# Layer 1's q and k in a two-layer fp32 kernel: dense products placed in strips by transfers, and one group's squares on ScalarE

## The chip, the cores and the metric

The kernel runs on one core of a Trainium2 chip. The metric is device time in microseconds from launch to end; lower is better. Three runs of the kernel before gave 1683.4, 1684.3 and 1684.37 us, median 1684.3. A profile page describes one further execution.

The engines have short names here. PE is TensorE (PEld its weight loads), DVE is VectorE, ACT is ScalarE, POOL is GpSimd, and SP is the engine whose queue issues nearly all transfers. PSUM is the memory into which PE writes its products.

## The reference

The input is x, 16 images of 512 tokens with 128 features, all fp32. Two layers follow each other. Both normalise, and both add an attention branch and a feed-forward branch to x:

```
xn = layernorm(x)
x  = x + linear_attention(xn) + mixture_of_experts(xn)      # layer 0
xn = layernorm(x)
x  = x + chunked_attention(xn) + channel_mix(xn)            # layer 1
```

Layer 0's attention is linear and causal, with 16 heads of 8 features and rotary positions. Its mixture of experts sends each token to 2 of 8 experts (128 -> 512 -> 128, with squared relu between) and adds a shared expert of the same shape.

Layer 1's attention is what the change is about:

```
q, k, v = xn @ W_qkv.T           # 16 heads of 8 features
for each chunk of 64 queries:    # keys up to the chunk's end
    p   = softmax(q k^T / sqrt(8))
    p   = p * (0.5 + 0.5 * gate(sum of p));  p = p / sum(p)
    out = p v
```

## The kernel before

**An order planned at build time.** The code does not run its loops in order. Generators describe the work; each call on an engine records an operation, and `Program.run` lays the operations out in an order with a list scheduler: it keeps a clock for each of the five engines, prices each operation by `COSTS` and by simple rules in `Program.call` (80 ns for an issue on SP, with an assumed landing 2 us later plus bytes at 250 GB/s), and emits what can start first, the lower index first among those. What is emitted is the fixed order of each engine. So changed work or a changed price moves the order of everything after it. All recorded operations have one line in the profile, L259, and groups are told apart by the names of their tiles. `Base` records who writes and reads a tile, `Slots` the buffers of a tag.

**Stages.** The 16 images go in five groups of 3, 4, 4, 3 and 2 (`GROUPS`). For each group, `dispatch` normalises and routes, and POOL scatters the token rows to their experts' slots in DRAM; `slot_tiles` fetches an expert's weights for each tile of 128 slots (`wf` and `wp`, 256 KB each, four buffers each) and computes hidden and output rows; `layer0` does linear attention and the shared expert; `layer1` does layer 1 image by image. These chains are woven together, so that experts and layer 0 of one group lie beside layer 1 of the group before.

**Experts' tiles** (`hidden`): a product `hg_ps`, a relu on ACT into `hg`, the square of `hg` in place, and the second product `yg_ps`. The square runs on POOL for the first pair of a quad and on DVE for the second; in group 0 always on DVE.

**Layer 1 of one image b.** `head(b)` loads x1, adds the experts' rows to it, normalises it into `xp`, runs `channel_mix` and `values`, and then `operands` for the first half of the heads (u=0). `body(b)` runs `weighted` for u=0 with `operands` of u=1 beside it, then `weighted` for u=1 with `head(b+1)` beside it.

A matmul here contracts over at most 32 rows for each of four strips of the PE array. A strip j holds two heads (16 rows of features), then rows that carry the running maximum and the mask. So `operands` wants q and k in strips of 32 partitions with 16 rows of data: `wqk1` is padded with zero columns accordingly, one product for each u and for each of q and k (`qk`), and DVE adds the constant rows while it moves the product out of PSUM: one addition for `qa`, and two for `ka` (one for each head of a pair, with `parity` clearing the other head's rows). Then come the scores `sc` in five units, whose maxima DVE takes into `maxima`; PE transposes these (`mx`), and DVE subtracts them from `qa` in place. `weighted` computes `st` from `ka` and `qa`, ACT the exponential `ex`, and PE the product `o` with the values. The tags `qa` and `ka` have two buffers. In group 0, `layer0` runs images 0 and 1 side by side, and the second borrows these buffers (`LENT`).

Of the kernel before, what the change touches and what calls it, by code (L numbers as in the profile page):

```python
# [29 lines left out]
F32 = mybir.dt.float32  # L30
# [6 lines left out]
P = 128  # L37
# [15 lines left out]
def slot_count(gt):  # L53
# [29 lines left out]
_CONST = (  # L83
    ("ident", P), ("cos", NT * 4), ("sin", NT * 4), ("blocks", 8 * (PAIR + 2)), ("pick", 4),
    ("causal", P), ("rank", E), ("upper", P), ("ones", P), ("tile", SLOT_TILES),
    ("aug_q", T), ("aug_k", 2 * T), ("parity", 2),
)


# [68 lines left out]
class Base:  # L158


    def __init__(self, slots, make):
        self.slots, self.make, self.tile = slots, make, None
        self.writers, self.readers = [], []
        self.left, self.free_at, self.users = 0, 0.0, []

    def made(self):
# [58 lines left out]
class Program:  # L225
# [21 lines left out]
    def call(self, name, api, method, args, kw):  # L247
        views = [a for a in (*args, *kw.values()) if isinstance(a, View)]
        o = kw.get("out", args[0] if args else None)
        writes = [o.base] if isinstance(o, View) else []  # L250
        reads = [v.base for v in views if v is not o]
        n = math.prod(o.shape[1:]) if isinstance(o, View) else 0
        later = 0.0

        def made(a):
            return a.made() if isinstance(a, View) else a

        def emit():
            return getattr(api, method)(*map(made, args), **{k: made(a) for k, a in kw.items()})  # L259

        if name == "PE":
            later = 60.0
            form = (args[1].shape[0], o.shape[0])
            if method == "transpose":
                cost = 112.0
            elif args[1].shape[0] == 32:
                cost = max(0.425 * n, 56.0)
            elif o.shape[0] == 32:
                cost = max(0.425 * n, 56.0)
            else:  # L270
                cost = max(1.68 * n, 224.0)
        elif method == "dma_start":
            cost, later = 80.0, 512.0 * n
        else:
            form = method if (name, method) in COSTS else None
            if name == "DVE" and method in ("tensor_scalar", "tensor_scalar_min", "tensor_scalar_max"):
                form = "fast"
            if method in ("tensor_reduce", "bn_stats"):
                n = math.prod(args[1].shape[1:])
            least, each = COSTS[name, form]  # L280
            cost = least + each * n
            if kw.get("func", args[2] if len(args) > 2 else None) == AF.Sqrt:
                cost += 2600.0
        op = self.add(name, emit, reads, writes, cost, later)
        if name == "PE":
            (self.unit_of[0] if self.unit_of else op).form = form
        return op

    def add(self, name, emit, reads, writes, cost, later=0.0):
        if self.unit_of is not None:  # L290
            if self.unit_of == []:
                self.unit_of.append(self._new(name, None, 0.0, 0.0))
            op = self.unit_of[0]
            part = Op(name, emit, 0.0, 0.0, op.index)
            op.parts.append(part)
            op.cost += cost
        else:
            part = op = self._new(name, emit, cost, later)
        for base in reads:
            op.needs.update(base.writers)  # L300
        for base in writes:

            op.needs.update(o for o in base.writers if o.engine != "SP" or name != "SP")
            op.needs.update(base.readers)
        for base in reads:
            base.readers.append(op)
        for base in writes:
            if base.readers:
                base.writers, base.readers = [], []
            base.writers.append(op)  # L310
        op.needs.discard(op)
        op.bases.update(reads, writes)
        op.wrote.update(writes)
        return part
# [172 lines left out]
def two_layers(ctx: ExitStack, tc: tile.TileContext, x, small, const, w_fc, w_proj, out):  # L487
# [22 lines left out]
    def big(name):  # L510
        return ps_big.tile([P, 2, 512], F32, tag="big", name=name)
# [6 lines left out]
        i.behind = [(first, mybir.DependencyClass.NoSync)]  # L518


    const_sb = fixed.tile([P, _CONST_N], F32, tag="const", name="const_sb")
    small_sb = fixed.tile([P, _STAYS_N], F32, tag="small", name="small_sb")

    wfc_s = fixed.tile([P, FF], F32, tag="wfc_s", name="wfc_s")
# [13 lines left out]
    lo = _CONST_AT["aug_q"][0]  # L538
    SP.dma_start(const_sb[:, 0:lo], const[:, 0:lo])
    raw = {}  # L540
    for name in ("wqkv0", "wqk1"):
        program.lag = 400 if name == "wqk1" else 0
# [3 lines left out]
    for names in (_STAYS[:2], _STAYS[2:]):  # L546
# [4 lines left out]
    lo = _CONST_AT["aug_q"][0]  # L551
    SP.dma_start(const_sb[:, lo:], const[:, lo:])
    program.lag = 250
    SP.dma_start(wfc_s, w_fc[:, E, :])
    SP.dma_start(wpj_s, w_proj[:, E, :, :])
# [2 lines left out]
    def c_(name):  # L558
        lo, hi = _CONST_AT[name]
        return const_sb[:, lo:hi]  # L560
# [19 lines left out]
    aug_k = c_("aug_k").rearrange("p (o t) -> p o t", o=2)  # L580
# [541 lines left out]
    def slot_tiles(g):  # L1122
# [41 lines left out]
        def hidden(xgT, ws, q, pair):  # L1164
            ph = big(f"hg_ps_{g}_{q}_{pair}")
            for ii, (wf, _) in enumerate(ws):
                i = 2 * pair + ii
                for f in range(NF):
                    M.matmul(
                        ph[:, ii, f * P : (f + 1) * P], wf[:, f * P : (f + 1) * P],  # L1170
                        xgT[:, i * P : (i + 1) * P], start=True, stop=True,
                    )
            h = p2.tile([P, 2, FF], F32, tag="hid", name=f"hg_{g}_{q}_{pair}", bufs=4)
            o = h[:, 0 : len(ws), :]
            S.activation(o, ph[:, 0 : len(ws), :], AF.Relu)

            (V if pair or g == 0 else G).tensor_tensor(o, o, o, ALU.mult)
            return h

        def project(h, ws, n):  # L1180
# [110 lines left out]
            )  # L1291
        return vp

    def operands(xT, b, u):
# [20 lines left out]
        yield  # L1315
        mx = maxima
        for i, unit in enumerate(QUERIES):
# [192 lines left out]
    def head(b):  # L1510

        if not 0 <= b < B:
            return None
        x1 = p2.tile([P, NT, D], F32, tag="x1", name=f"x1_{b}")
        assert passed["x1", b].base.writers
        SP.dma_start(x1.rearrange("p t d -> p (t d)"), passed["x1", b])
        yield from combine(x1, b)
        xp = p2.tile([P, T + 1], F32, tag="xp", name=f"xp_{b}", bufs=2)
        G.memset(xp[:, 0:1], 0.0)
        yield from layernorm_T(x1, xp[:, 1 : T + 1], f"1_{b}", "xn1", 1)  # L1520
        yield
        base = yield from channel_mix(x1, xp, b)
        yield
        vp = values(xp[:, 1 : T + 1], b)
        yield
        qm, ka = yield from operands(xp[:, 1 : T + 1], b, 0)
        return xp, base, vp, qm, ka

    def body(b, state):


        xp, base, vp, qm, ka = state
        o0, (qm, ka) = yield from weighted(
            qm, ka, vp, b, 0, operands(xp[:, 1 : T + 1], b, 1), 2
        )
# [64 lines left out]
def _constants():  # L1600
# [15 lines left out]
    parity = np.zeros((4, 32, 2), f)  # L1616
    for o in range(2):
        aug_k[:, PAIR + o, o] = 1.0
        parity[:, o * DH : (o + 1) * DH, o] = 1.0
# [4 lines left out]
    c["parity"] = parity.reshape(P, 2)  # L1624
# [66 lines left out]
```

## Time and profile before

| what | value |
|---|---|
| runs | 1683.4, 1684.3, 1684.37 us (median 1684.3) |
| profiled execution | 1683.13 us, span of its instructions 1681.3 us |
| mean granted clock of PE | 0.973 |
| PE busy | 1566.0 us (93%), 14503 matmul passes |
| DVE busy | 1220.5 us (73%) |
| ACT busy | 763.4 us (45%) |
| POOL busy | 405.0 us (24%) |
| transfers | 167.78 MB, mean 100 GB/s |

The span runs from the first to the last instruction; the time of a run includes what lies around it (1.8 us in the profiled execution). A row of a group reads: line, engine, operation, out<-in, shapes and count, then the busy time in us and the mean ns of one, then the idle time of the engine just before these instructions and what ended it. A row of the timeline reads: start in us, duration in us, engine, line, operation, tiles, count. SPq is SP's queue issuing transfers; its durations are those of the issue, not of the transfer. A row of stages gives the busy time of each engine between two points of the span, with counts, the granted clock, the busy share of the DMA engines and GB/s.

### The profile page before, as it was taken

What the parts mean: (1) busy time and instruction counts of PE and PEld (TensorE: products, weight loads), DVE (VectorE), ACT (ScalarE), POOL (GpSimd) and SP (SyncE); (2) the same over time, 40 slices, a digit from 0 to 9 for tenths busy, and PEclk for the clock granted to TensorE, in tenths of its full rate; (3) what the DMA queues carried; (4) which work ended last, traced back from release to release, by engine and by line L of the source; (5) the groups of instructions that cost most, each with busy time, mean ns of one, the idle gap of its engine ahead of it and who ended that gap; (6) DMA issues with size and microseconds to landing.
All of it is one profiled execution on the core that took longest, in us unless ns stands there. A gap on an engine that the chain in (4) does not pass through costs nothing.

```text
span 1681.3 us, 36447 instructions
## 1 busy us (share of the span) xinstructions
PE 1566.0 (93%) x14503; PEld 1027.3 (61%) x14503; DVE 1220.5 (73%) x2520; ACT 763.4 (45%) x1175; POOL 405.0 (24%) x389
## 2 busy tenths in 40 slices
PE   5898889999999999999999999999999999999996
PEld 3687766576756566665766656656665566555443
DVE  7876269767479875977678884968587867676773
ACT  3343334535445554445445553453545543534434
POOL 2404362162115211251014321140115010104000
PEclk8899999999999999999999999999999999999888
DMA  5377857143433532332332332313133223011000
GB/s 173 110 219 223 247 185 218 47 136 98 125 96 94 162 93 69 116 95 75 95 98 81 103 95 79 103 60 114 49 93 89 63 72 101 8 44 29 19 1 13
DMA packets 155129, 167.78 MB, mean 100 GB/s; under 512 B 13264, under 2 KB 100688, under 8 KB 154960
## 3 DMA queue, kind: packets, MB, share of 16 engines
q1 hardware_dynamic: 146768, 148.67, 29.7%
q0 software_dynamic: 8192, 16.79, 3.2%
q8 instruction: 114, 1.87, 0.4%
q14 instruction: 55, 0.45, 0.1%
HBM read 123.59 MB, written 41.81 MB: 98 GB/s over the span
## 4 chain that ended last, share of the span: by engine, by line
PE 55%; DVE 13%; ACT 3%; issue 1%; ACTq 0%; DVEq 0%
PE sc L259 11%; PE o L259 10%; PE st L259 8%; PE yg_ps L259 5%; DVE maxima L259 4%; PE hg_ps L259 4%; PE y L259 4%; PE qk L259 3%; PE h_ps L259 2%; ACT ex L259 1%; PE ho_a L259 1%; PE qkv L259 1%; PE oh_a L259 1%; PE mx L259 1%; PE cm_r L259 1%
## 5 line engine op out<-in xcount | busy, mean ns | idle before, releaser
L259 DVE TENSOR_REDUCE maxima<-sc 128x2 f32<-128x768 f32 (+2 forms) x448 | 385.4, 913 | 74.4 <-PE sc L259 71.4
L259 ACT ACTIVATE ex<-st 128x1024 f32<-128x1024 f32 x320 | 312.4, 1025 | 183.2 <-PE st L259 174.0
L259 PE MATMUL sc<-ka,qa 32*128 32x512 f32 (+2 forms) x1792 | 214.5, 518 | 7.5 <-DVE maxima L259 3.9
L259 PE MATMUL st<-qa,ka 32*128 32x384 f32 (+3 forms) x2048 | 209.3, 467 | 9.3 <-ACT ex L259 4.6
L259 DVE TENSOR_TENSOR am<-sc,const_sb 128x1024 f32<-128x1024 f32 x128 | 151.3, 1217 | 81.5 <-PE sc L259 76.6
L259 PE MATMUL yg_ps<-wp,hg 128*128 128x128 f32 x1304 | 182.1, 283 | 18.4 <-DVE hg L259 6.3
L259 PEld LDWEIGHTS yg_ps<-wp,hg 128*128 128x128 f32 x1304 | 160.0, 192 | 61.3 <-issue 32.1
L1091 POOL DMA_INDIRECT rows<-xn,pl_slot x128 | 131.4, 1026 | 224.0 <-DVE pl_slot L259 46.8
L259 PE MATMUL hg_ps<-xgT,wf 128*128 128x128 f32 x1304 | 176.1, 280 | 9.0 <-DMA wf<-in_w_fc 3.6
L1110 POOL DMA_INDIRECT back<-results,pl_slot x128 | 127.2, 994 | 220.2 <-PE st L259 45.6
L259 PEld LDWEIGHTS hg_ps<-xgT,wf 128*128 128x128 f32 x1304 | 158.7, 193 | 32.9 <-issue 13.4
L259 PE MATMUL o<-ex,vpad 128*32 128x512 f32 (+3 forms) x2048 | 175.7, 445 | 1.1 <-ACT oT_a L259 0.6
L259 PEld LDWEIGHTS st<-qa,ka 32*128 32x128 f32 x2048 | 103.6, 185 | 78.1 <-issue 27.0
L259 ACT ACTIVATE hg<-hg_ps 128x1024 f32<-128x1024 f32 x84 | 84.0, 1000 | 137.0 <-PE hg_ps L259 123.0
L259 PEld LDWEIGHTS sc<-ka,qa 32*128 32x128 f32 x1792 | 90.5, 188 | 69.0 <-issue 21.4
L259 POOL TENSOR_TENSOR hg<-hg 128x1024 f32<-128x1024 f32 x34 | 65.1, 1914 | 276.4 <-ACT hg L259 276.1
L259 PEld LDWEIGHTS o<-ex,vpad 128*32 128x32 f32 x2048 | 52.5, 109 | 88.0 <-issue 66.0
L259 DVE TENSOR_TENSOR hg<-hg 128x1024 f32<-128x1024 f32 (+1 forms) x50 | 58.4, 1168 | 59.3 <-ACT hg L259 45.7
L259 ACT COPY oTs<-o 128x256 f32<-128x256 f32 (+1 forms) x96 | 42.6, 444 | 125.4 <-PE o L259 113.6
L259 PE MATMUL sc<-q0m,k0T 32*128 32x256 f32 x1024 | 82.1, 412 | 3.3 <-ACT ex L259 1.4
L259 ACT COPY yg<-yg_ps 128x256 f32<-128x256 f32 x84 | 31.0, 369 | 112.5 <-PE yg_ps L259 77.0
L259 PE MATMUL o<-am,vpad 128*32 128x128 f32 x2048 | 77.0, 277 | 1.2 <-DVE am L259 0.9
(189 smaller groups left out, 2216.8 us busy)
## 6 DMA issues: line engine op xcount, KB each, us to landing
wf<-in_w_fc SPq DMA_DIRECT2D x163, 256.0 KB
wp<-in_w_proj SPq DMA_DIRECT2D x163, 256.0 KB
results<-yg SPq DMA_DIRECT2D x79, 128.0 KB
xg<-rows SPq DMA_DIRECT2D x37, 256.0 KB
rows<-zeros SPq DMA_DIRECT2D x2, 2496.0 KB
x_in<-in_x SPq DMA_DIRECT2D x16, 256.0 KB
x<-x SPq DMA_DIRECT2D x16, 256.0 KB
out<-rr SPq DMA_DIRECT2D x16, 256.0 KB
```

The costliest lines, as they stand in the source:

```text
L259: return getattr(api, method)(*map(made, args), **{k: made(a) for k, a in kw.items()})
L1091: i = nc.gpsimd.indirect_dma_start(out=rows.made()[:, :], out_offset=bass.IndirectOffsetOnAxis(ap=slot.made(), axis=0), in_=row.made(), in ...
L1110: "POOL", lambda: nc.gpsimd.indirect_dma_start(out=o.made(), out_offset=None, in_=results.made()[:, :], in_offset=bass.IndirectOffsetOnAxi ...
```

## The change

- `dense`, called once for each image right after the normalisation, makes q and k of all 16 heads with an unpadded `wqk1` (128 x 128 for each): two products in place of four. ACT copies both from PSUM into SBUF tiles `q1` and `k1`, with one buffer each; `q1` shares the buffer of tag `xn1` with the normalised rows of the head.
- The strips `qa` and `ka` are made once for each u (`make_strips`), filled from the constants in DRAM, and stay for all images. For every image and u, `operands` issues 12 transfers on SP's queue, from SBUF to SBUF: four of 16 rows for `qa` and eight of 8 rows for `ka`, each row 2 KB. DVE's additions are gone, and `parity` with them.
- The maxima are no longer subtracted in place: the result goes to a new tile `qm`.
- In group 0, the squares of the experts' hidden tiles run on ACT, as an activation right behind the relu.
- The constants for `qa` and `ka` are no longer loaded into `const_sb` at the start.
- Two rules of the planner change: a transfer's assumed bytes follow its number of partitions, and a tile that is written again by several writers makes each of them wait for the readers before (`Base.before`).

```diff
-    const_sb = fixed.tile([P, _CONST_N], F32, tag="const", name="const_sb")
+    const_sb = fixed.tile([P, _CONST_AT["aug_q"][0]], F32, tag="const", name="const_sb")
...
-            cost, later = 80.0, 512.0 * n
+            cost, later = 80.0, 4.0 * n * (o.shape[0] if isinstance(o, View) else P)
...
+            op.needs.update(base.before)
...
             if base.readers:
+                base.before = base.writers + base.readers
                 base.writers, base.readers = [], []
...
-    wqk1 = fixed.tile([P, 4, 4, 32], F32, tag="wqk1", name="wqk1")
-    G.memset(wqk1, 0.0)
-    given1 = raw["wqk1"].rearrange("p (su j o e) -> p su j o e", su=4, j=4, o=2)
-    for o in range(2):
-        V.tensor_copy(wqk1[:, :, :, o * DH : (o + 1) * DH], given1[:, :, :, o, 0:DH])
+    wqk1 = fixed.tile([P, 2, P], F32, tag="wqk1", name="wqk1")
+    given1 = raw["wqk1"].rearrange("p (h e) -> p h e", e=32)
+    V.tensor_copy(
+        wqk1.rearrange("p s (h e) -> p (s h) e", e=DH), given1[:, :, 0:DH]
+    )
...
-            (V if pair or g == 0 else G).tensor_tensor(o, o, o, ALU.mult)
+            if g == 0:
+                S.activation(o, o, AF.Square)
+            else:
+                (V if pair else G).tensor_tensor(o, o, o, ALU.mult)
...
-        ps = big(f"qk1_{b}_{u}")
+    def make_strips():
+        for u in range(2):
+            qa = p2.tile([P, T], F32, tag="qa", name=f"qa_{u}")
+            ka = p2.tile([P, 2, T], F32, tag="ka", name=f"ka_{u}")
+            (lo, hi), (klo, khi) = _CONST_AT["aug_q"], _CONST_AT["aug_k"]
+            first = [
+                SP.dma_start(qa, const[:, lo:hi]),
+                SP.dma_start(ka.rearrange("p o t -> p (o t)"), const[:, klo:khi]),
+            ]
+            strips.append((qa, ka, first))
+
+    def dense(xT, b):
+
+        if not strips:
+            make_strips()
+        ps = big(f"qk1_{b}")
         for i in range(2):
-            M.matmul(
-                ps[:, i, :], wqk1[:, 2 * i + u, :, :].rearrange("p j e -> p (j e)"), xT,
-                start=True, stop=True,
-            )
-        qa = p2.tile([P, T], F32, tag="qa", name=f"qa_{b}_{u}")
-        V.tensor_tensor(qa, ps[:, 0, :], c_("aug_q"), ALU.add)
-        ka = p2.tile([P, 2, T], F32, tag="ka", name=f"ka_{b}_{u}")
-        for o in range(2):
-            V.scalar_tensor_tensor(
-                ka[:, o, :], ps[:, 1, :], c_("parity")[:, o : o + 1], aug_k[:, o, :],
-                ALU.mult, ALU.add,
-            )
+            M.matmul(ps[:, i, :], wqk1[:, i, :], xT, start=True, stop=True)
+        q = p2.tile([P, T], F32, tag="xn1", name=f"q1_{b}", bufs=1)
+        k = p2.tile([P, T], F32, tag="k1", name=f"k1_{b}", bufs=1)
+        S.copy(q, ps[:, 0, :])
+        S.copy(k, ps[:, 1, :])
+        return q, k
+
+    def operands(qk, b, u):
+
+        q, k = qk
+        qa, ka, first = strips[u]
+        for j in range(4):
+            at, r = u * P // 2 + j * PAIR, 32 * j
+            rows = [SP.dma_start(qa[r : r + PAIR, :], q[at : at + PAIR, :])]
+            for o in range(2):
+                rows.append(SP.dma_start(
+                    ka[r + o * DH : r + (o + 1) * DH, o, :], k[at + o * DH : at + (o + 1) * DH, :]
+                ))
+            for i in rows if first else ():
+                after(i, first)
+        strips[u] = (qa, ka, [])
...
-        V.tensor_tensor(qa, qa, pm, ALU.subtract)
+        qm = p2.tile([P, T], F32, tag="qm", name=f"qm_{b}_{u}")
+        V.tensor_tensor(qm, qa, pm, ALU.subtract)
         yield
-        return qa, ka
+        return qm, ka
...
         yield from layernorm_T(x1, xp[:, 1 : T + 1], f"1_{b}", "xn1", 1)
         yield
+        qk = dense(xp[:, 1 : T + 1], b)
+        yield
         base = yield from channel_mix(x1, xp, b)
```

More of the change, by code (lines that the diff above doesn't have):

```diff
@@ L85 @@
     ("causal", P), ("rank", E), ("upper", P), ("ones", P), ("tile", SLOT_TILES),
-    ("aug_q", T), ("aug_k", 2 * T), ("parity", 2),
+    ("aug_q", T), ("aug_k", 2 * T),
 )
@@ L162, in __init__ @@
         self.slots, self.make, self.tile = slots, make, None
-        self.writers, self.readers = [], []
+        self.writers, self.readers, self.before = [], [], []
         self.left, self.free_at, self.users = 0, 0.0, []
@@ L537, in two_layers @@
     x_in = {b: load_x(b, "x_in", 2) for b in range(2)}
-    lo = _CONST_AT["aug_q"][0]
-    SP.dma_start(const_sb[:, 0:lo], const[:, 0:lo])
+    SP.dma_start(const_sb, const[:, 0 : _CONST_AT["aug_q"][0]])
     raw = {}
@@ L550, in two_layers @@
         SP.dma_start(small_sb[:, slo:shi], small[:, lo:hi])
-    lo = _CONST_AT["aug_q"][0]
-    SP.dma_start(const_sb[:, lo:], const[:, lo:])
     program.lag = 250
@@ L579, in two_layers @@
     sin = c_("sin").rearrange("p (t d) -> p t d", d=4)
-    aug_k = c_("aug_k").rearrange("p (o t) -> p o t", o=2)
     program.lag = 200
-    wqk1 = fixed.tile([P, 4, 4, 32], F32, tag="wqk1", name="wqk1")
-    G.memset(wqk1, 0.0)
-    given1 = raw["wqk1"].rearrange("p (su j o e) -> p su j o e", su=4, j=4, o=2)
-    for o in range(2):
-        V.tensor_copy(wqk1[:, :, :, o * DH : (o + 1) * DH], given1[:, :, :, o, 0:DH])
+    wqk1 = fixed.tile([P, 2, P], F32, tag="wqk1", name="wqk1")
[3 more added lines that the diff above has]
+    )
     program.lag = 1000
@@ L1292, in values @@
         return vp
-    def operands(xT, b, u):
-        ps = big(f"qk1_{b}_{u}")
-        for i in range(2):
-            M.matmul(
-                ps[:, i, :], wqk1[:, 2 * i + u, :, :].rearrange("p j e -> p (j e)"), xT,
-                start=True, stop=True,
-            )
-        qa = p2.tile([P, T], F32, tag="qa", name=f"qa_{b}_{u}")
-        V.tensor_tensor(qa, ps[:, 0, :], c_("aug_q"), ALU.add)
-        ka = p2.tile([P, 2, T], F32, tag="ka", name=f"ka_{b}_{u}")
-        for o in range(2):
-            V.scalar_tensor_tensor(
-                ka[:, o, :], ps[:, 1, :], c_("parity")[:, o : o + 1], aug_k[:, o, :],
-                ALU.mult, ALU.add,
-            )
+    strips = []
+    def make_strips():
[12 more added lines that the diff above has]
+        ps = big(f"qk1_{b}")
+        for i in range(2):
+            M.matmul(ps[:, i, :], wqk1[:, i, :], xT, start=True, stop=True)
[17 more added lines that the diff above has]
+        strips[u] = (qa, ka, [])
         yield
@@ L1525, in head @@
         yield
-        qm, ka = yield from operands(xp[:, 1 : T + 1], b, 0)
-        return xp, base, vp, qm, ka
+        qm, ka = yield from operands(qk, b, 0)
+        return qk, base, vp, qm, ka
     def body(b, state):
-        xp, base, vp, qm, ka = state
+        qk, base, vp, qm, ka = state
         o0, (qm, ka) = yield from weighted(
-            qm, ka, vp, b, 0, operands(xp[:, 1 : T + 1], b, 1), 2
+            qm, ka, vp, b, 0, operands(qk, b, 1), 2
         )
@@ L1615, in _constants @@
     aug_q, aug_k = np.zeros((4, 32, T), f), np.zeros((4, 32, 2, T), f)
-    parity = np.zeros((4, 32, 2), f)
     for o in range(2):
         aug_k[:, PAIR + o, o] = 1.0
-        parity[:, o * DH : (o + 1) * DH, o] = 1.0
     for t in range(NT):
@@ L1623, in _constants @@
     c["aug_q"], c["aug_k"] = aug_q.reshape(P, T), aug_k.reshape(P, 2 * T)
-    c["parity"] = parity.reshape(P, 2)
     inv = (f(10000.0) ** (-np.arange(4, dtype=f) / f(4))).astype(f)
```

## The prediction

> **What bounds the kernel now.** I read the page's busy shares and slices first, then the windows by stage, then the groups, PE's waits, and the timeline where the changed lines run.
>
> ```profile
> PE 1566.0 (93%) x14503; PEld 1027.3 (61%) x14503; DVE 1220.5 (73%) x2520; ACT 763.4 (45%) x1175; POOL 405.0 (24%) x389
> ...
> PE   5898889999999999999999999999999999999996
> ...
> DVE  7876269767479875977678884968587867676773
> ```
>
> ```profile
> core 0: us, PE busy (x) PEld busy (x) DVE busy (x) ACT busy (x) POOL busy (x), PEclk, DMA share, GB/s
> 252.00:336.00 84.00, 78.20 (x689) 51.39 (x686) 71.17 (x182) 42.78 (x64) 16.67 (x15) 0.96 0.44 132
> 336.00:1512.00 1176.00, 1137.31 (x10764) 734.93 (x10756) 880.52 (x1693) 556.88 (x844) 275.81 (x252) 0.99 0.30 90
> 1512.00:1596.00 84.00, 78.48 (x702) 41.43 (x696) 60.07 (x125) 39.00 (x51) 18.67 (x18) 0.94 0.08 24
> 1596.00:1682.00 86.00, 67.74 (x548) 33.28 (x544) 47.41 (x99) 33.08 (x45) 2.92 (x3) 0.83 0.03 7
> ```
>
> TensorE sets the time. From 336 to 1512 us it is busy 1137 of 1176 us (97%) while DVE is at 75% and ACT at 47%. Work taken from PE there shortens the kernel nearly one for one, unless PE then waits for something; work taken from DVE or ACT counts only where PE waits for them, and from 336 to 1512 PE's named waits are 2 us or less each.
>
> ```profile
> L259 PE MATMUL qk<-xp,wqk 128*128 128x512 f32 x128 | 63.5, 600 | 0.1
> ...
> L259 DVE SCALAR_TENSOR_TENSOR ka<-qk,const_sb 128x512 f32<-128x512 f32 x64 | 45.6, 742 | 0.0
> L259 DVE TENSOR_TENSOR qa<-qk,const_sb 128x512 f32<-128x512 f32 x32 | 22.0, 689 | 21.6 <-PE qk L259 21.4
> L259 DVE TENSOR_TENSOR hg<-hg 128x1024 f32<-128x1024 f32 x45 | 55.0, 1221 | 56.1 <-ACT hg L259 42.5 <-issue 13.5
> L259 ACT COPY xgT<-xgT_ps 128x512 f32<-128x512 f32 x37 | 21.7, 588 | 26.3 <-PE xgT_ps L259 19.9 <-issue 6.1
> ```
>
> ```profile
> 874.87 1.88 PE L259 MATMUL qk<-xp,wqk 128*128 128x512 f32 x4
> ...
> 2.34 0.43 SPq L259 DMA_DIRECT2D raw_wqkv<-in_small  x1
> 2.81 0.43 SPq L259 DMA_DIRECT2D small_sb<-in_small  x1
> 3.29 0.43 SPq L259 DMA_DIRECT2D wfc_s<-in_w_fc  x1
> ...
> 1577.52 0.33 SPq L259 DMA_DIRECT2D x<-xs  x1
> 1579.59 0.33 SPq L259 DMA_DIRECT2D x<-x  x1
> ```
>
> The product of layer 1's q and k is 128 passes. The SP rows give two prices: back-to-back issues stand 0.48 us apart, and a copy that needs the previous one landed (x<-x after x<-xs, on an idle queue) is issued 2.07 us later.
>
> **1. Half of the q/k product goes.** Before, each image makes two padded products for each half u: 16 x 2 x 2 x 2 passes = 128. After, q and k are made once, 64 passes. Four passes take 1.88 us, of which the pipeline's drain is about 0.16 (0.60 for one pass less its 0.43 interval); 0.43 us each. 64 x 0.43 = 27.5 us. By half the group's busy time it would be 31.7; I take the interval, since drains lie beside the next matmul. **-27.5.**
>
> **2. DVE loses the placing.** 22.0 + 45.6 = 67.6 us, and group 0's squares, 15 of 1.22 and one of 0.69 = 19.0. DVE is no bound; it pays only through PE's waits for DVE, some 10 us from 336 to 1512, few of them in front of these rows. Between 0 and -6: **-2.**
>
> **3. ACT gains.** 32 copies from PSUM, 128x512, at 0.588 = 18.8 us; group 0's squares 15 x 1.03 + 0.60 = 16.0; and two more table loads of 1.28 in the order of the new kernel's instructions. In 336 to 1512 ACT has 619 us free; behind the copies stand exponentials and gate activations, 1.2 us late per image, for which PE waits 4 us in all in that stage. In group 0's stage (84 to 252) PE waited 6.3 us for DVE's squares; on ACT the square follows its relu without a hand-over, but weights arriving late (3.6 us of waits) would take up part. Between -6 and +4: **-1.**
>
> **4. Start.** The 769 KB constant load leaves the first queue (x_in behind it is some 3.5 us earlier; DVE waits 3.7 us for it at 16 us), wqk1's memset (0.52, behind POOL's other memsets) and one of two 0.35 us copies go. Later 1.5 MB of constants for the strips go out around 84 us, when batch 1's borrowed buffers are read out, ahead of the first rows of the experts; at 219 GB/s that is 7 us of DMA, for a transfer that has 2 us to spare before PE's transposes at 94.7. Each -3 to +3: **0.**
>
> **5. The strips come by transfers.** Per image and half 4 transfers of q (32 KB) and 8 of k (16 KB), 384 issues, all on SP's one queue, in front of which and behind which the experts' weights stand. In the new order q's 4+4 strips of both halves go first, then 8 of ka for u=0: PE's first score waits for the 16th issue. After the last product: hand-over 0.2, copy 0.59, 16 x 0.48 = 7.7, landing 2.3 (2.07 and a little traffic) = 10.8 us. Before, it was DVE's 0.69 + 0.74.
> A rule speaks against it: the Trainium skill, "DMA: Bandwidth & Descriptors", section "Rules for kernel authors", has transfers below 64 KB coalesced, and "SBUF — State Buffer", section "The DMA setup-cost knee", gives a fixed 2 us plus bytes at 436 GB/s. Paid one after another, 16 x 2.05 = 33 us, about 20 us beyond the average cover below, 16 times: +320 us, some 1975 us in all. The rows at 2.34 to 3.29 show issues overlapping at 0.48 us, so the fixed part is paid once at the end; I use that. The strips are spread over eight completion semaphores and each waits for the eighth before it; 8 x 0.48 = 3.8 us is above a landing, so that wait should be empty.
> Cover: PE's work between the latest matmul that the strips hang on and the first score, by the new order, each matmul at its group's busy time per instruction. For u=0, images 0 to 15: 4.9, 12.8, 12.1, 9.6, 11.0, 16, 21, 13.7, 13.9, 15, 14.9, 7.6, 23, 17.6, 7.4, 7.6 us. Short of 10.8: image 0 by 5.9, 3 by 1.2, 11, 14, 15 by 3.2 to 3.4, together 17. For u=1 only ka's 8 strips come late, after image b-1's last st: 0.9 + 3.8 + 2.3 = 7 us against 13 to 26, covered. q shares the one buffer of tag xn1, so the next image's normalised rows wait for q's 8 transfers; these go out an image earlier: 0.
> Weights queued behind strips: SP's 16 issues hold the next wf back by 7 us; counted in the same way (landing 3.3 for 256 KB) three places are short, images 2, 7 and 8, by 5.2, 2.3, 3.6 = 11; what is late next is hg_ps, then the relu and yg_ps. Sum 28. The same count made on the old order finds 7 us of late weights where PE's waits show 3.6 to 4.6, because PE's small gaps stretch every cover; so I take about half: **+14**, bounds 0 and 30.
> PE gets 94 more wait instructions (426 for 332). PE's unnamed gaps from 336 to 1512, some 24 us, over some 240 waits are at most 0.1 us each: 0 to 9, **+2**, most of them find their semaphore long met.
>
> **Sum:** -27.5 - 2 - 1 + 0 + 14 + 2 = -14.5 on the profiled execution's 1683.1 (span 1681.3) = 1668.6. The median of the runs is 1.2 above that execution: **1670**, and so against 1684.3.
>
> **Rivals.**
> - *Slower: SP's queue becomes the bound.* One mechanism: a strip costs more than 0.48 us on SP, since each first waits for the eighth before it, and landings behind two 256 KB weight loads are 3.4 us or more. Place: in front of each image's first score of u=0. With c us for a strip the need is 3.1 + 16c. At 0.63 the shortfalls and the late weights, halved as above, eat the gain; at 0.9 the need is 17.5, shortfalls 81 + weights 31 = 112, halved 62: 1684.3 - 28.5 + 62 = 1718. For it: the DMA engines are busy for 0.30 of the middle stage already, and only the last images' strips meet an idle queue. Against: nothing in SP's rows shows 0.9 for a lone issue.
> - *All strips hidden.* The covers stretch with PE's gaps, short transfers issue faster than 0.48. Then only -28.5: 1656. Against: image 0's 4.9 us.
> - *The change does nothing to the time.* The saved passes only uncover DVE's maxima (DVE 85 to 88% busy in some 84 us stretches) or the tail's chain (PE is 79% busy after 1596, clock 0.83, with image 15's longer way to its scores): 1684.
>
> **How the numbers follow.** Chances: likeliest 0.50 (its own range 1661 to 1679), hidden 0.15, slower 0.25, nothing 0.10. A measurement of this kernel tells about 0.2%, 3.4 us, from no change. Faster: 0.50 + 0.15 and a little of the last = 0.67; within 0.2%: 0.06; slower: 0.25 and the rest = 0.27. Range 1654 (passes at busy time, strips hidden) to 1700 (the slower rival at 0.75 us a strip); beyond it 0.06 below and 0.12 above.
>
> **What would show it.** Step 1: qk x64 and some 32 us busy. Step 2, 3: no qa<-qk and ka<-qk on DVE, ACT near 800. Step 5: waits of PE sc for DMA ka<-k1, around 10 us in all, largest in image 0 (near 245 us) and in the last two; hg_ps for wf in images 2, 7, 8. It is wrong if those waits total over 30 us, if strips on SP stand more than 0.6 us apart, or if PE's share falls below 90%.

## The result

The changed kernel takes 1743.95 us (median of 4 runs, 1739.29 to 1750.64) against 1684.34 us before on the same chip: ratio 1.0359, 95% interval 1.0327 to 1.0391. It is 60 us slower where 14 us less had been forecast, and lies outside the range. The profiled execution took 1742.91 us, its span 1741.1.

The page of the changed kernel: busy time and share of each engine with its instructions, then TensorE's busy tenths and its granted clock in 40 slices.

```profile
PE 1593.5 (92%) x14439; PEld 1040.0 (60%) x14439; DVE 1137.2 (65%) x2407; ACT 796.2 (46%) x1225; POOL 404.4 (23%) x388
...
PE   5899889999899998999989898999999999999986
...
PEclk8899989999999999999998998989999999999988
```

There are 64 passes fewer, and yet PE is busy for 27.5 us longer than before (1593.5 for 1566.0). The share hides the loss, since a matmul at half clock counts as busy for nearly twice as long (in this trace the passes of hg_ps follow each other in 112 ns at full clock and in 214 at half, by the median). The row of PE now has 8s in its middle, where before it had 9s from slice 7 on.

The window of the middle stage (columns as in the prediction):

```profile
core 0: us, PE busy (x) PEld busy (x) DVE busy (x) ACT busy (x) POOL busy (x), PEclk, DMA share, GB/s
336.00:1512.00 1176.00, 1103.37 (x10291) 711.15 (x10283) 793.88 (x1551) 552.96 (x845) 274.20 (x247) 0.97 0.33 94
```

In the middle stage PE gets 10291 passes done in the 1176 us in which it did 10764 before, and its mean clock is 0.97 for 0.99. DVE, which the change relieved, is at 68% for 75%. PE's own waits, longest first (us in total, times, longest):

```profile
PE hg_ps L260 <- DMA wf<-in_w_fc: 26.1, 11, 8.6
PE ln_ps L260 <- DVE xn L260: 23.1, 5, 10.0
PE sc L260 <- DMA ka<-k: 9.0, 10, 1.9
```

The row of ln_ps belongs to the start and is there in every kernel of this study. The first row was, in the kernel before:

```profile
PE hg_ps L259 <- DMA wf<-in_w_fc: 3.6, 3, 1.8
```

The strips themselves hold PE back for 9.0 us. The experts' weights, for which nothing was changed, hold it back for three times as much. The timeline of image 2's strips shows how (start, duration, what, and in brackets the idle time before it and what ended it):

```profile
448.04 0.58 ACT L260 COPY q<-qk 128x512 f32<-128x512 f32 x1 [3.44 <-PE qk L260]
...
448.65 5.00 SPq L260 DMA_DIRECT2D qa<-q  x8
...
453.75 5.43 SPq L260 DMA_DIRECT2D ka<-k  x8
...
460.51 0.37 SPq L1145 DMA_DIRECT2D wf<-in_w_fc  x1
...
463.45 2.05 PE L260 MATMUL hg_ps<-xgT,wf 128*128 128x128 f32 x8 [8.58 <-DMA wf<-in_w_fc]
```

SP is occupied with the strips' issues from 448.65 to 459.2. After them it reads the expert's number (1.3 us with what goes with it) and issues that expert's weights, which land 2.9 us later. PE, whose next product in its order needs them, stands from 454.9 on for 8.58 us. The weights are not longer on their way than before: from issue to landing wf takes 3.07 us by the median of the middle stage, in the kernel before as in a second profile of the changed kernel (`changed_again` below). They go out late. The windows around that place add the second half of the price:

```profile
core 0: us, PE busy (x) PEld busy (x) DVE busy (x) ACT busy (x) POOL busy (x), PEclk, DMA share, GB/s
451.00:454.80 3.80, 3.80 (x69) 2.77 (x68) 0.00 (x0) 2.68 (x5) 0.00 (x0) 1.00 0.23 56
454.80:463.40 8.60, 0.07 (x4) 0.00 (x0) 2.36 (x2) 0.00 (x0) 0.00 (x0) 0.79 0.27 76
463.40:466.60 3.20, 3.15 (x10) 2.21 (x10) 0.00 (x0) 0.00 (x0) 0.00 (x0) 0.50 0.85 249
```

During the stall the granted clock falls, and the first 3.2 us of work after it run at 0.50. A stall of 8.6 us thus costs some 10 (an estimate: half of those 3.2 us on top).

A smaller wait came with the change as well. DVE may not write the next image's normalised rows (`xn`) before q's transfers have left the buffer that the two share. For this DVE stands 36.8 us in 7 waits, and what is queued behind on DVE comes late, twice for PE too (4.4 and 1.9 us). One of the two:

```profile
671.43 0.60 DVE L260 TENSOR_SCALAR xn<-x,ln_mv,ln_rstd 128x128 f32<-128x128 f32 x2 [5.87 <-DMA ka<-k]
...
675.40 3.40 PE L260 MATMUL yg_ps<-wp,hg 128*128 128x128 f32 x16 [4.40 <-DVE o0n L260]
```

(The row names ka, whose transfers follow q's on the same semaphores; the buffer is q's.) In sum PE's waits for DVE did not grow: 23.0 us from 252 to 1600 us, for 25.6 before.

**Where the 60 us went.** PE's span splits into three parts: its gaps; half of the time that it is busy while the trace grants it half clock (the price of the clock); and the rest of its busy time, which is the work at full clock. The second is an estimate, since a matmul at half clock takes not quite twice as long. Some 4 us behind PE's last matmul are left out; they are the same in all kernels. In us, each row from one profiled execution:

| | work at full clock | price of the clock | gaps |
|---|---|---|---|
| before | 1533.1 | 32.9 | 111.1 |
| changed | 1524.8 | 68.7 | 143.5 |
| difference | -8.3 | +35.8 | +32.4 |

So the wanted gain is small, the gaps took 32 us, and the clock, for which the prediction had no term, took 36.

### The profile page after: what moved, and what is told of

The parts are those of the page before. It is cut to its first block, busy times and chain, and to the rows that moved or that the text cites. A ratio compares the mean times of both kernels' runs of the same rounds, so it can differ in the third digit from the quotient of the medians.

```text
span 1741.1 us, 37030 instructions
## 1 busy us (share of the span) xinstructions
PE 1593.5 (92%) x14439; PEld 1040.0 (60%) x14439; DVE 1137.2 (65%) x2407; ACT 796.2 (46%) x1225; POOL 404.4 (23%) x388
## 4 chain that ended last, share of the span: by engine, by line
PE 70%; DVE 12%; ACT 7%; issue 4%; SPq 4%; DMA 3%; POOL 0%; ACTq 0%; DVEq 0%; POOLq 0%
PE sc L260 13%; PE o L260 12%; PE st L260 8%; PE yg_ps L260 8%; PE hg_ps L260 7%; PE y L260 5%; DVE maxima L260 4%; SPq L260 3%; PE h_ps L260 3%; PE qkv L260 2%; DMA wf<-in_w_fc 2%; PE qk L260 2%; ACT ex L260 2%; PE ho_a L260 1%; PE cm_v L260 1%
## 5 line engine op out<-in xcount | busy, mean ns | idle before, releaser
L260 PE MATMUL sc<-ka,qa 32*128 32x512 f32 (+2 forms) x1792 | 236.4, 529 | 17.9 <-DMA ka<-k 9.0
L260 PE MATMUL st<-qm,ka 32*128 32x384 f32 (+3 forms) x2048 | 209.2, 470 | 8.3 <-DVE maxima L260 3.7
L260 PE MATMUL hg_ps<-xgT,wf 128*128 128x128 f32 x1304 | 183.6, 285 | 29.7 <-DMA wf<-in_w_fc 26.1
L260 PEld LDWEIGHTS hg_ps<-xgT,wf 128*128 128x128 f32 x1304 | 162.5, 195 | 59.2 <-issue 27.4
L1090 POOL DMA_INDIRECT rows<-xn,pl_slot x128 | 127.7, 998 | 228.4 <-DVE pl_slot L260 67.0
L260 PE MATMUL o<-ex,vpad 128*32 128x512 f32 (+3 forms) x2048 | 179.2, 455 | 0.5 <-ACT ex L260 0.3
L260 PEld LDWEIGHTS sc<-ka,qa 32*128 32x128 f32 x1792 | 96.5, 191 | 92.6 <-issue 35.6
L260 PEld LDWEIGHTS st<-qm,ka 32*128 32x128 f32 x2048 | 103.9, 187 | 76.9 <-issue 26.5
L260 PE MATMUL sc<-q0m,k0T 32*128 32x256 f32 x1024 | 86.1, 419 | 6.7 <-ACT ex L260 3.4
```

The costliest lines, as they stand in the source:

```text
L1090: i = nc.gpsimd.indirect_dma_start(out=rows.made()[:, :], out_offset=bass.IndirectOffsetOnAxis(ap=slot.made(), axis=0), in_=row.made(), in ...
```

## The experiments

Two theories were set against each other at first. Q: the 384 issues of strips hold SP's queue, weights queued behind them come late, PE stalls and its clock falls. O: something else in the change costs the time (the new order, ScalarE's copies and squares, the table loads), and the transfers are hidden. Each run of this section was made beside runs of the kernel before on the same chip, whose median was between 1675 and 1679 us; ratios are against that.

### once: strips for the first image alone

```diff
-        for j in range(4):
+        for j in range(4) if b == 0 else ():
```

> The changed kernel without the strips' transfers of images 1 to 15: only image 0's 24 are issued, so that layer 1's scores of all later images are made from image 0's q and k (that part of the computation is left out). Everything else of the change stays: dense product, copies on ACT, qm, squares on ACT, the order by the same planner. Theory Q (the 384 issues on SP's queue hold back the experts' weights, PE stalls and its granted clock falls): 1648 to 1662 us, that is the 27 us of the product and a little, wf waits of PE under 6 us, clock 0.97 or more. Theory O (the new order, the copies on ACT and the squares are what costs, the transfers are hidden): 1715 us or more.

Measured: 1653.9 us, 0.9887 (0.9836 to 0.9939). Work 1511.1, clock 26.8, gaps 103.1 (the profiled execution was the fastest of the four, 1646.8 us). PE's waits for wf:

```profile
PE hg_ps L260 <- DMA wf<-in_w_fc: 1.3, 2, 0.7
```

Everything in the change but the repeated transfers is therefore worth 21 us of gain (10 to 27 by the interval). Theory O falls: copies, squares, product and the new tiles stay in this kernel. It also means that the transfers cost more than the loss against the kernel before shows: counted from `once`, the changed kernel is 4.5 to 4.8% slower.

### dummy: the same number of transfers in the kernel before, to DRAM

```diff
+        spare = memory.tile([P, T], F32, tag=f"spare{b}_{u}", name=f"spare_{b}_{u}")
+        for j in range(4):
+            r = 32 * j
+            SP.dma_start(spare[r : r + PAIR, :], qa[r : r + PAIR, :])
+            for o in range(2):
+                SP.dma_start(
+                    spare[r + PAIR + o * DH : r + PAIR + (o + 1) * DH, :],
+                    ka[r + o * DH : r + (o + 1) * DH, o, :],
+                )
```

> The kernel before, whole, with 384 further transfers of the change's sizes (4 of 16 rows and 8 of 8 rows per image and half, from qa and ka to a DRAM area that nobody reads) at the place where the change has its strips, and with the change's rule for a transfer's assumed bytes. Theory Q: 1715 to 1760 us, PE waits for wf over 15 us, clock below 0.96. Theory O: 1684 to 1695 us.

Measured: 1679.42 us, 1.0019 (0.9999 to 1.0039). Theory Q missed: it had asked for 35 us or more. The timeline of SP in this kernel says why the load was not the same:

```profile
447.44 1.73 SPq L259 DMA_DIRECT2D spare<-qa  x4
449.26 3.27 SPq L259 DMA_DIRECT2D spare<-ka  x8
```

Twelve issues take 5.1 us here. In the changed kernel the sixteen of image 2 took 10.5. By the median of all neighbours the issues stand 0.344 us apart, against 0.676 for the strips. Two explanations were left: the price of an issue (same rows, another target), or that nobody waits for these transfers. They are told apart below.

### price: the planner's price of a strip

The order on SP's queue is written by the planner, which counts an issue as 80 ns.

```diff
+            if isinstance(o, View) and o.shape[0] <= PAIR:
+                cost = 650.0
```

> The changed kernel with one number of the planner changed: an issue of 16 rows or fewer on SP is priced 650 ns and not 80, what the trace of the changed kernel shows from one strip to the next. The instructions are the same, their order is laid out anew. Theory Q: the weights are planned around the strips, 1670 to 1700 us, PE waits for wf under 10 us, clock 0.96 or more. Theory O: 1725 us or more.

Measured: 1697.52 us, 1.0120 (1.0078 to 1.0162). Work 1523.8, clock 47.8, gaps 118.9. The waits of PE on weights and strips are nearly gone:

```profile
PE hg_ps L260 <- DMA wf<-in_w_fc: 2.2, 4, 0.8
PE sc L260 <- DMA ka<-k: 1.2, 2, 0.8
```

In SP's timeline weights now go out between the strips of one image:

```profile
440.47 1.41 SPq L260 DMA_DIRECT2D ka<-k  x2
443.20 0.37 SPq L1147 DMA_DIRECT2D wf<-in_w_fc  x1
...
444.22 0.56 SPq L260 DMA_DIRECT2D qa<-q  x1
```

Not a transfer or its size was changed, only its place in the order, and two thirds of the loss against the kernel before went away; counted from `once` it is half (2.4% are left of 4.5 to 4.8). Against the kernel before, what is left is 8 us of gaps and 15 us of clock. The gaps are many small waits for DVE and ACT (28.7 and 26.9 us from 252 to 1600 us, for 25.6 and 22.4 before); one of 3.5 us stands behind DVE's wait for q's buffer. Why the clock falls more often is not shown.

### act: strips on ScalarE's queue

```diff
-            rows = [SP.dma_start(qa[r : r + PAIR, :], q[at : at + PAIR, :])]
+            rows = [S.dma_start(qa[r : r + PAIR, :], q[at : at + PAIR, :])]
...
-                rows.append(SP.dma_start(
+                rows.append(S.dma_start(
...
+            if name == "ACT":
+                cost = 500.0
```

> The changed kernel with the strips' transfers issued by ACT on its own queue instead of SP (planner's price 500 ns each), so that nothing stands in front of the weights. Theory Q: PE's waits for wf fall below 6 us; the time is 1665 to 1700 us unless ACT, which now issues 384 times about 0.65 us = 250 us, holds back the exponentials, then up to 1730 with waits of PE for ex over 20 us. Theory O: 1730 us or more with waits for neither.

Measured: 1705.16 us, 1.0172 (1.0130 to 1.0215). An issue costs ScalarE about as much as SP, and now ScalarE's own work stands behind it. PE's waits for ScalarE sum to 38.5 us from 252 to 1600 us, for 22.4 before; those for ex alone to 14.6, where over 20 had been expected for a time above 1700. Two of the rows:

```profile
PE sc L260 <- ACT ex L260: 7.4, 10, 2.1
...
PE cm_v L260 <- ACT xnT L260: 5.6, 1, 5.6
```

The timeline shows two issues and what stood behind them, an activation on whose result PE's cm_v product depends:

```profile
456.94 1.32 ACTq L260 DMA_DIRECT2D ka<-k  x2
458.30 0.60 ACT L260 ACTIVATE xk<-cm_k 128x512 f32<-128x512 f32 x1 [3.01 <-DMA qa<-q]
```

Weights are no longer late (1.9 us), and the kernel is still slower. So the time of issuing costs on ScalarE too, though less.

### changed_again: the changed kernel once more

> The changed kernel once more, beside the others of this call. All theories: 1.033 to 1.039 of the kernel before, PE's waits for wf some 26 us, its waits for ka some 9 us, half-clock time near 174 us.

Measured: 1735.25 us, 1.0333 (1.0291 to 1.0375). PE's waits for wf 28.5 us, for ka 7.4 us, half-clock time 193 us, a little more than expected. The loss is there again. Work, clock and gaps are 1520.9, 79.8 and 137.3, for 1524.8, 68.7 and 143.5 in the first profile: two executions of one kernel differ by 4, 11 and 6 us, so differences of that size between kernels say little.

### once_spare: the same transfers, and nobody waits

```diff
-            rows = [SP.dma_start(qa[r : r + PAIR, :], q[at : at + PAIR, :])]
+            rows = [SP.dma_start((qa if b == 0 else spare[0])[r : r + PAIR, :], q[at : at + PAIR, :])]
...
-                    ka[r + o * DH : r + (o + 1) * DH, o, :], k[at + o * DH : at + (o + 1) * DH, :]
+                    (ka if b == 0 else spare[1])[r + o * DH : r + (o + 1) * DH, o, :], k[at + o * DH : at + (o + 1) * DH, :]
```

> The changed kernel; from image 1 on, its strips are sent in the same 12 transfers for each half, of the same rows and row length, to a spare pair of strips that nothing reads, so layer 1's scores of later images use image 0's q and k. SP's issues stay, PE's scores wait for none of them. Theory Q (the strips' issues hold SP's queue, 0.62 to 0.68 us each, and the experts' weights behind them come late): 1.020 to 1.036 of the kernel before, waits of hg_ps for wf 15 us or more, half-clock time above 130 us. Theory D (the loss hangs on PE's scores waiting for the strips, the issues alone harm nothing): 0.985 to 0.997, wf waits below 8 us, as in the run whose strips were sent once.

Measured: 1728.2 us, 1.0307 (1.0277 to 1.0338). (For room, image 0's strips are one pair here for both halves.) Beside `once` it differs in its transfers, which gate no engine but for the reuse of the buffers of q and k, and it is 4% slower. Beside the changed kernel only the scores' waits are gone, and the loss is nearly whole.

```profile
PE hg_ps L260 <- DMA wf<-in_w_fc: 33.6, 12, 11.9
...
PE sc L260 <- DMA ka<-k: 0.5, 2, 0.3
```

Theory D, that the loss hangs on the scores' waits, is out: the transfers cost as much when nobody reads what they bring. One wait on them is left, that for q's buffer: DVE stands 38.0 us for it in 6 waits, and three waits of PE behind it are 8.9 us. So this run alone does not separate the issues from that wait; the next one does, in which no buffer of q is reused.

### dummy_sbuf: the dummies once more, with SBUF as the target

```diff
+            SP.dma_start(spare[r : r + PAIR, :], qa[r : r + PAIR, 0:8])
...
+                    ka[r + o * DH : r + (o + 1) * DH, o, 0:8],
```

> The kernel before, with 12 transfers of 16 and 8 rows for each image and half, from SBUF to SBUF as the strips are but 32 bytes a row, which nothing reads. Theory Q, if an issue's price hangs on the target being SBUF and not on bytes: cadence 0.6 to 0.68 us as in the strips (0.34 in the run whose dummies went to DRAM), time 1.008 to 1.035, since the bursts are 12 issues long and not 16 to 24; wf waits 8 to 20 us. If the price hangs on bytes: cadence below 0.45 and 1.000 to 1.005. Theory D: 1.000 to 1.005 whatever the cadence.

Measured: 1710.17 us, 1.0205 (1.0180 to 1.0230). PE's waits for wf are somewhat above the 8 to 20 us expected:

```profile
PE hg_ps L259 <- DMA wf<-in_w_fc: 22.0, 11, 4.7
```

The timeline of SP:

```profile
457.61 2.47 SPq L259 DMA_DIRECT2D spare<-qa  x4
460.19 5.50 SPq L259 DMA_DIRECT2D spare<-ka  x8
```

The twelve issues take 8.1 us where those to DRAM took 5.1, and the median distance is 0.669 us. The rows here have 32 bytes, against 2 KB to DRAM: the price follows the target and not the bytes. That explains the miss of `dummy`, and it puts 2% of loss into the kernel before without any other part of the change: no new product, no copies, no wait of the scores and none of DVE for a strip's transfer.

### squares: ScalarE's squares alone

```diff
-            (V if pair or g == 0 else G).tensor_tensor(o, o, o, ALU.mult)
+            if g == 0:
+                S.activation(o, o, AF.Square)
+            else:
+                (V if pair else G).tensor_tensor(o, o, o, ALU.mult)
```

> The kernel before with group 0's squares on ScalarE, nothing else. The prediction gave this part -6 to +4 us: 0.996 to 1.003. Theory Q: within that, the loss is none of it. A theory that the squares on ScalarE cost a good part of the loss (relu and square in one chain, table loads): 1.010 or more.

Measured: 1675.06 us, 0.9986 (0.9972 to 1.0000). A gain of some 2 us, if any, and none of the loss.

### eight_strips and eight_priced: 256 issues for 384

```diff
-            rows = [SP.dma_start(qa[r : r + PAIR, :], q[at : at + PAIR, :])]
-            for o in range(2):
-                rows.append(SP.dma_start(
-                    ka[r + o * DH : r + (o + 1) * DH, o, :], k[at + o * DH : at + (o + 1) * DH, :]
-                ))
+            rows = [
+                SP.dma_start(qa[r : r + PAIR, :], q[at : at + PAIR, :]),
+                SP.dma_start(ka[r : r + PAIR, :, :], k[at : at + PAIR, :, :]),
+            ]
...
-        S.copy(k, ps[:, 1, :])
+        for o in range(2):
+            S.activation(k[:, o, :], ps[:, 1, :], AF.Copy, scale=c_("parity")[:, o : o + 1])
```

> The changed kernel with 8 transfers for each image and half in place of 12, all of 16 rows: ScalarE writes k twice, once with each second head set to zero (one copy more per image), and one transfer carries both planes; the tile qm has one buffer, for room. Theory Q (the loss goes with the time that the strips' issues hold SP's queue): 256 issues at 0.51 to 0.6 us are 130 to 155 us in place of 250, so about half the loss is left: 1.005 to 1.022 of the kernel before, waits of hg_ps for wf 6 to 16 us, half-clock time 110 to 150 us. A rival in which any fine-grained strip on SP does the harm, whatever the count: 1.027 or more.

> As the run with 8 transfers, and the planner counts an issue of up to 16 rows as 650 ns in place of 80. Theory Q: as the price took a little over half of the loss with 12 transfers (1.036 to 1.012), 0.996 to 1.008 here, wf waits below 8 us. Rival as before: 1.010 or more.

Measured: 1700.15 us, 1.0144 (1.0114 to 1.0173), and with the price 1669.8 us, 0.9953 (0.9939 to 0.9967). The issues stand 0.632 us apart. Without the price, work, clock and gaps are 1515.3, 52.7, 124.3; PE waits 4.9 us for wf, below the 6 to 16 expected, and 6.0 for ka. With it they are 1514.4, 40.6, 111.9, and PE waits 2.4 us for wf.

A third fewer issues take away over half of the loss against the kernel before (from `once` it is over 40%), and with the price the kernel is faster than the changed one and 0.5% faster than the one before, where the interval excludes no change. It was a little better than the expected 0.996.

### padded_rows and padded_mended: strips read whole from DRAM

```diff
+        S.dma_start(qd.rearrange("(g r) t -> g r t", r=32)[:, 0:PAIR, :], q)
+        S.dma_start(
+            kd.rearrange("(g r) t -> g r t", r=32)[:, 0:PAIR, :], k.rearrange("p o t -> p (o t)")
+        )
...
+        SP.dma_start(qa, qd[u * P : (u + 1) * P, :])
+        SP.dma_start(ka.rearrange("p o t -> p (o t)"), kd[u * P : (u + 1) * P, :])
```

> q and k made once as in the changed kernel, but the placing goes through DRAM: k is copied out of PSUM twice with each second head set to zero, q and k are written on ScalarE's queue into padded rows in DRAM whose constants lie there already (2 transfers of 128 rows an image), and SP reads each strip tile whole, 4 transfers of 128 rows an image in place of 24; the maxima are subtracted in place as before. Theory Q: SP's issues for strips are 64 at some 0.33 us = 21 us, no weights come late beyond 5 us in all, and the gain of the halved product shows: 0.985 to 0.998 of the kernel before. Rival: two landings one after the other (some 3 us each) and 24 MB more traffic cost PE's first scores more than the gain, waits of sc for ka above 20 us, and 1.003 or more.

Measured: 2008.53 us, 1.1985 (1.1949 to 1.2021), a miss of 20%. But the rival's mark was not there either: PE's waits for ka are 11.2 us, below its 20. PE's gaps sum to 301 us; the largest named part is in front of oh_a, at the end of an image. And SP stood twice for q's way out, the longer time 56 us:

```profile
PE oh_a L260 <- DVE o1n L260: 73.0, 13, 9.3
```

```profile
SPq L260 <- DMA qd<-q: 108.1, 2, 56.2
```

This pointed to the order. The planner multiplied the free size of the destination by 128 partitions, and for a padded write that free size holds the 16 rows of a head pair too: 8 times the bytes. The second kernel counts them from the shape, and has the constants for the padded rows go out later.

```diff
-            cost, later = 80.0, 512.0 * n
+            cost, later = 80.0, 4.0 * n * (o.shape[0] if isinstance(o, View) else P)
...
+                i.needs.update(passed["xnT", 8 if s else 3].base.writers)
```

> The padded rows in DRAM once more, with two things mended that made the last order bad: the planner had counted a write of q or k into padded rows at 8 times its bytes (it multiplied the 16 rows of a head pair by 128 partitions), so that it believed the strips landed 25 to 60 us late, and it sent the 3 MB of constants for the padded rows ahead of the first loads; now the bytes are counted from the shape, and the constants go out after the fourth and the ninth image's normalised rows. Theory Q (SP's issues are the loss; with 64 of 0.33 us there is none): PE's gaps back to 105 to 125 us, half-clock time below 125 us, 0.988 to 1.004 of the kernel before. Rival (the way over DRAM itself, two landings and 24 MB more, is what cost 20%): 1.05 or more, waits of sc for ka above 20 us.

Measured: 1680.91 us, 1.0013 (0.9997 to 1.0029). A wrong figure in the planner and constants sent too early had cost 328 us; which of them how much was not tried. Work 1516.2, clock 48.5, gaps 108.3. The way over DRAM costs little issue time (on SP 0.33 us for a qa and 0.42 for a ka, 64 of them; on ScalarE 0.59, 32 of them) and hardly a wait (ka 3.1 us). Still it stops short of the 1.1% that `once` gained. Work and gaps differ by 5 us each, which is within the scatter above; the clock takes 22 us more, and for that no cause is shown.

## Why the prediction was wrong

**Step 1, the halved product: right on its group, too large as a gain.** The group of the product, of the changed kernel:

```profile
L260 PE MATMUL qk<-xp,wqk 128*128 128x512 f32 x64 | 32.7, 624 | 0.9 <-ACT ex L260 0.9
```

32.7 us for the 32 forecast, 30.8 less than before. PE's work at full clock fell by 22.0 us in `once`, 19.2 in `once_spare`, 17 to 19 with 8 transfers and with `padded_mended`, but by only 8.3 in the changed kernel (12.2 in `changed_again`). So -27.5 was 5 to 10 us too much even where nothing is late. Why the changed kernel's work shrank by less than that is open.

**Steps 2 and 3, DVE and ACT: right.** DVE lost 83.3 us (86.6 forecast), and PE's waits for it fell by 2.6 us (252 to 1600 us). ACT came to 796.2, near 800. The squares were measured by themselves: -2 us, within -6 to +4.

**Step 4, the start: right.** Up to 252 us PE runs 1832 passes, for 1821 before.

**Step 5, the strips: here it failed, in the price of an issue, in the halving, in a wait put at nothing, and in the clock, for which there is no term.** Of the 74 us between forecast and measured time, 36 are the clock, 19 the gaps (32.4 for the 13 in the sum) and 19 the work of step 1.

- *0.48 us for an issue.* Measured 0.676 from one strip to the next (0.625 in the row of an 8-row issue, 0.51 to 0.58 for 16 rows, and a hand-over). The 0.48 was read from issues of 128 rows from DRAM at the start, which in the middle of the kernel take 0.34. It was the nearest row that the trace of before had, but no transfer in it went from SBUF to SBUF with few rows. `dummy` and `dummy_sbuf` show the target to be worth a factor of two. The bound of the range assumed 0.75, so the price alone was inside it.
- *Weights queued behind the strips: the places were right.* The prediction named images 2, 7 and 8, with 5.2, 2.3 and 3.6 us. PE waits for wf there 8.58, 4.84 and 6.81 us, 20.2 of the 26.1. With 0.676 for 0.48, sixteen issues hold the queue 3.1 us longer, and the same count gives 8.3, 5.4 and 6.7. So the count was sound and the price of the issue was wrong.
- *The halving.* It was taken from the old order's late weights, where the same count had found 7 us against 3.6 to 4.6. For these three waits nothing is to be halved: the full count, at the measured price, is what came.
- *The scores' waits: right in sum by luck.* They came at the five images that were named (0, 3, 11, 14, 15), 9.0 us for the halved 8.5. But at 0.676 the count gives 38 us, halved 19. The low price and covers that were counted too short cancelled.
- *q's shared buffer, put at 0* because q's transfers "go out an image earlier". DVE stands for them 36.8 us in 7 waits, of which at least 6.3 us reach PE.
- *No term for the clock.* PE's price of the clock went from 32.9 to 68.7 us, more than the gaps' own +32.4. From 250 to 1590 us the trace grants PE half clock for 95.6 us, 34.1 before, in 15 phases for 5. Each of the four gaps of over 4 us in that stretch is followed by such a phase within 5 us of its start. The Trainium skill has a rule that would have called for this term: "TensorE: Matmul & The Clock Gate", section "HAM oscillation — how this bites in real kernels", warns of PE gaps above some 3.4 us. But these four phases are 27.2 us of the 95.6; the other eleven follow gaps of 0.3 to 2.1 us, and the five of before gaps of 0.4 to 1.4. So the rule explains at most 9 us of the difference in price (PE is busy for 18 of the 27.2 us), and what sets the others off is open.

The rule that the prediction weighed and turned down, that transfers below 64 KB be coalesced ("DMA: Bandwidth & Descriptors", "Rules for kernel authors"), pointed the right way: 256 issues for 384 took 2 of the 3.5 percent. Its reason did not apply: the fixed 2 us do overlap, as the prediction said (the strips land some 2.0 us after their issue, not one after another); what is paid for each transfer is the issue.

**The rivals.** *SP's queue becomes the bound* had the mechanism, and put the break-even at 0.63 us a strip; the measured 0.676 is beyond it. It looked first in front of the scores, halved the late weights and had no clock, and so its size was wrong: by its own working 0.676 gives about the time before (38 us of scores and 20 of weights, halved 29, against 28.5 saved), not 60 us more. Its sum for 0.9 has a slip: half of 112 is 56, which makes 1712 and not 1718. *All strips hidden* is `once` in effect: 1656 forecast against 1684, a gain of 28.5, measured 21. The marks given for being wrong came: waits for strips and weights of 35 us (30 was the bound), strips over 0.6 us apart. The third, PE's share below 90%, did not come, since the lost clock keeps the share up.

## What to carry to other kernels

Cost a transfer three times: on the queue that issues it, in what stands behind it on that queue, and where its data are needed; an in-order queue that carries weights is a shared engine, and 384 issues of 0.65 us are 250 us of it. A planner's price for an issue is part of the kernel: the same transfers cost 1.2% in place of 3.3 to 3.6% when their price was true, and a wrong figure for bytes, with constants sent too early, cost 20%. Where PE is the bound, count gaps and clock apart from the work, since the busy share reads 92% in a kernel that lost 3.6%.

## What the runs showed of the hardware that was not expected

- An issue on SP of few rows from SBUF to SBUF takes longer than one of 128 rows: 0.625 us for 8 rows, 0.51 to 0.58 for 16, 0.34 for the weights' 128 rows. To DRAM, 8 rows take 0.26 to 0.29 and 16 rows 0.31 to 0.41. With rows of 32 bytes the price to SBUF is the same as with 2 KB. ScalarE's queue has about the same price (0.54 for 16 rows, 0.63 for 8). Why few rows into SBUF take longer was not tried.
- PE falls to half clock after gaps of under 2 us too, in every kernel here. `price` and `padded_mended` have 8 us more and 3 us less of gaps than before, and yet a price of the clock that is 15 us higher in both. Whether the places of the gaps matter more than their sum, no run here separates.
